# Moving the first layer's expansion matmuls from four-pass float32 to one-pass float32r, with the operand carried through DRAM

## The chip, the core and the metric

The kernel runs on one core of a Trainium2 chip. Its time is the device time of one execution, in microseconds (us). The engines of the core work from separate instruction queues: PE (TensorE, the matmuls), PEld (the loading of a matmul's stationary operand, which can lie beside a matmul), DVE (VectorE), ACT (ScalarE), POOL (GpSimd) and SP (SyncE, which here only issues DMA transfers). SBUF is the on-chip memory of 128 partitions, PSUM the memory that matmuls write to, DRAM the memory outside. The kernel before takes 4007.41 us (median of three runs, 4005.51 to 4009.65).

## The reference

A batch of 8192 samples of 8 x 16 x 16 float32 values goes through four residual layers. Each normalises the samples in groups of two channels, applies a linear map and adds the result to what came in. The change touches layer 0 alone, whose map is a product of three small cores:

```python
def _L0_conv_ref(x, core0, core1, core2, bias):
    ...
    z = x.reshape(b, 1, sin[0], M_rest, 1)
    for k, c in enumerate(cores):
        z = jnp.einsum('bpmqr,rnms->bpnqs', z, c)
        ...
    return z.reshape(batch_shape + tuple(sout)) + bias

def reference(x, ...):
    x = x + _L0_conv_ref(_gn(x), L0_conv_core0, L0_conv_core1, L0_conv_core2, L0_conv_bias)
    x = x + _L1_conv_ref(_gn(x), ...)     # 3x3 convolution, batch norm, relu
    x = x + _L2_conv_ref(_gn(x), ...)     # quantised 3x3 convolution
    x = x + _L3_conv_ref(_gn(x), ...)     # 3x3 convolution with binarised weights
    return x
```

`core2` works on the last axis (16 values in, 16 values and 8 ranks out); `core0` and `core1` together map the other 128 values of a sample and the 8 ranks to 128 values.

## The kernel before

The batch is cut into 64 tiles of 128 samples; a tile is a [128, 2048] float32 array, and is worked on in four quarters of 32 samples. Layers 0 and 1 run together in a first stage of 256 quarters. In it every quarter has three groups of matmuls:

- `expand`, twice: the normalised x (`xn`, 16 rows for the last axis, two samples in 32 partitions) is the stationary operand, and `core2` is streamed past it. Result `pu`, in PSUM, copied by ACT to `u`.
- `main`: eight matmuls of 512 columns over `u`, one for each rank. Result `po`; DVE adds it to x.
- `conv1`: six matmuls of 128 columns, layer 1's convolution for the quarter six earlier. Results `pm` and `pc`.

```python
def expand(t, q, k):                       # before
    if k == 0:
        T[t]["u", q] = us[q % 2].rearrange("p (b n) -> p b n", b=QS)
    pu = ps_u.tile([P, 4, 2, 2 * R * W], F32, ...)          # ps_u holds one such buffer (4 banks)
    xv = T[t]["xn"].rearrange("p (n m) -> p n m", m=CH)
    for j in range(2):
        for i in range(4):
            rows = slice(32 * i, 32 * i + 32)
            pe.matmul(pu[:, i, j], xv[rows, (2 * q + k) * 2 + j],
                      core2[rows].rearrange("p a n -> p (a n)"), start=True, stop=True)
    act.copy(T[t]["u", q][:, 16 * k:16 * k + 16]..., pu...)

def main(t, q, between, n0=None):
    ...
    for r in range(R):                     # R = 8
        for f, args in between.get(r, ()):
            f(*args)                       # other steps, put between the matmuls
        pe.matmul(samples(po)[:, a:b], core01[:, r], u[:, a:b, r, :], start=(r == 0), stop=(r == R - 1))
    dve.tensor_tensor(x[:, cols], po, x[:, cols], ALU.add)

for n in range(NT * NQ):                   # the first stage, a quarter at a time
    ...
    at(0, tn < NT, expand, tn, qn, 0)      # the next quarter's expansion, first half, before matmul r = 0
    at(4, tn < NT, expand, tn, qn, 1)      # and second half, before matmul r = 4
    at1(0, conv1_input, LAG)               # POOL makes conv1's operand
    at1(6, conv1_scaled, LAG - 1)          # ACT's part of it
    if q == 0:
        ... norm_sums, norm_stats of tile t - 1; load_b(t + 3)
    elif q == 1:
        ... norm_b_square of tile t + 2; norm_apply of tile t - 1; load_t(t + 3)
    elif q == 2:
        ... norm_b_sums, norm_b_stats of tile t + 2
    else:
        ... add_bias of tile t + 3; norm_b_spread, norm_b_apply of tile t + 2
    at1(3, conv1_output, LAG + 1)          # DVE puts layer 1's output together
    main(t, q, steps, ...)
    conv1(*quarter_of(n, LAG))
```

Every compute engine keeps the order of the program. `xb` (x in the layout that `expand` needs) is loaded into three buffers `bs`; its normalised form goes to two buffers `xns`. Layer 3, at the end of the kernel, already uses one-pass products: there x is split into `hi` and `lo`, both float32r, and both are multiplied with weights that are exact in that format:

```python
def layer3(i, h):
    for m, t in enumerate(("hi", "lo")):
        for k in range(2):
            ...
            for n in range(3):
                pe.matmul(samples(pc[:, k]), L["sign3"][:, n], tv[:, :, n:n + W], ...)   # 512 columns, rows of 16 out of 18
```

Of the kernel before, what the change touches and what calls it, by code (L numbers as in the profile page):

```python
# [18 lines left out]
P = 128  # L19
C, H, W = 8, 16, 16  # L20
CH = C * H
# [11 lines left out]
class InOrder:  # L33
# [5 lines left out]
    def __getattr__(self, name):  # L39
        op = getattr(self.engine, name)  # L40

        def call(*args, **kwargs):
# [3 lines left out]


PACK0 = [("c0", R * C), ("c1", R * H), ("core2", 2 * R * W), ("bias0", W)]
PACK1 = [("w1", 9 * C), ("linb", C), ("gamma", 1), ("beta", 1), ("w2", 9 * C), ("w2all", C * C * 9), ("bias2", 1),
         ("w3", 9 * C), ("w3all", C * C * 9), ("bias3", 1)]  # L50


@with_exitstack
def tile_net(ctx: ExitStack, tc: tile.TileContext, xb, xt_in, pack0, pack1, out):
    nc = tc.nc
    NT = xt_in.shape[0]

# [3 lines left out]

    x1_d = [dram.tile([P, F], F32, name=f"x1_d{t}", tag=f"x1_d{t}") for t in range(NT)]
    y_d = [dram.tile([P, F], F32, name=f"y_d{t}", tag=f"y_d{t}") for t in range(NT)]
    x2_d = [dram.tile([P, F], F32, name=f"x2_d{t}", tag=f"x2_d{t}") for t in range(NT)]

    def load_pack(src, parts, pool, name):
        t = pool.tile([P, src.shape[1]], F32, name=name)
        nc.scalar.dma_start(t, src)
        views, at = {}, 0
        for key, n in parts:  # L70
            views[key] = t[:, at:at + n]
            at += n
        return views


    hold = ctx.enter_context(tc.tile_pool(name="hold", bufs=1))
    xs, bs, ys, xns, sqs = ([hold.tile([P, F], F32, name=f"{n}{k}") for k in range(m)]
                            for n, m in (("xs", 4), ("bs", 3), ("ys", 2), ("xn", 2), ("sq", 2)))
    us = [hold.tile([P, 2 * F], F32, name=f"u{k}") for k in range(2)]

    STAY = 4
    order2 = list(range(NT - STAY, NT)) + list(range(NT - STAY))
    y_stay = [bs[(NT - 3) % 3], bs[(NT - 2) % 3], bs[(NT - 1) % 3], ys[(NT - 1) % 2]]
    y_of = dict(zip(order2, y_stay))

    x_slots = ([xs[t % 4] for t in order2[:STAY]] + [xns[NT % 2]] + [us[0][:, h * F:(h + 1) * F] for h in range(2)]
               + [xns[(NT - 1) % 2]] + [us[1][:, h * F:(h + 1) * F] for h in range(2)] + y_stay[:3])
    y_slots = [ys[(NT - 1) % 2], ys[NT % 2]] + sqs
    T2 = [dict() for _ in range(NT)]

    def load2(i):
        T2[i]["x"] = x_slots[i % KEEP]
        T2[i]["y"] = y_stay[i] if i < STAY else y_slots[(i - STAY + 1) % len(y_slots)]
        if i >= STAY:
            nc.sync.dma_start(T2[i]["y"], y_d[order2[i]])
            nc.sync.dma_start(T2[i]["x"], x1_d[order2[i]])
# [1 line left out]

    first = ExitStack()
    const1 = first.enter_context(tc.tile_pool(name="const1", bufs=1))  # L100
    w0 = load_pack(pack0, PACK0, const1, "w0")
    ident = const.tile([P, P], F32, name="ident")
    make_identity(nc, ident)
    mhalf = const.tile([P, 64], F32, name="mhalf")
# [22 lines left out]

    core2 = w0["core2"].rearrange("p (a n) -> p a n", a=2)  # L130
    bias0_t = w0["bias0"]
    core01 = const1.tile([P, R, CH], F32, name="core01")
# [1 line left out]

    def late_constants(late):

        w = load_pack(pack1, PACK1, late, "w1")
        yield "load"

        scratch = ys[1]  # L140

        def band(wr, sh, dtype, name):

            acc, tmp = (scratch[:, k * 3 * CH:(k + 1) * 3 * CH].rearrange("p (k h) -> p k h", h=H) for k in range(2))
            b = (const1 if name == "1" else const).tile([P, 3, CH], dtype, name=f"band_{name}", tag=f"band_{name}")
            bv = b.rearrange("p k (c h) -> p (k c) h", c=C)
            wr = wr.rearrange("p (k n) -> p k n", k=3)
            for kh in range(3):
                wv = wr[:, kh, :].unsqueeze(2).to_broadcast([P, 3 * C, H])
                mv = sh[:, kh:kh + H].unsqueeze(1).to_broadcast([P, 3 * C, H])  # L150
                if kh == 0:
                    dve.tensor_tensor(acc, wv, mv, ALU.mult)
                    continue
                dve.tensor_tensor(tmp, wv, mv, ALU.mult)
                dve.tensor_tensor(bv if kh == 2 else acc, acc, tmp, ALU.add)
            L[f"band{name}"] = b

        for k in ("gamma", "beta", "bias2", "bias3"):
            L[k] = const.tile([P, 1], F32, name=k)
# [123 lines left out]
    with first as s:  # L283
# [14 lines left out]
        for t in x1n:  # L298
            pool.memset(t[:, :, 0:W + 2:W + 1], 0.0)

        def load_b(t):
            T[t]["xb"] = bs[t % 3]
            nc.sync.dma_start(T[t]["xb"], xb[t])

        def load_t(t):
# [28 lines left out]
            group_spread(spread0, T[t].pop("mvb"), W)  # L334

        def norm_b_apply(t, q=None):
            src = T[t]["xb"]
            if q in (None, 0):
                T[t]["xn"] = xns[t % 2]
            xn = T[t]["xn"]  # L340
            n = NB // 2 if q is None else NB // NQ
            for k, op, i in ((0, ALU.subtract, src), (1, ALU.mult, xn)):
                for a in range(0, NB, n) if q is None else [q * n]:
                    cols = slice(a, a + n)
                    dve.tensor_tensor(rows_b(xn)[:, cols], rows_b(i)[:, cols],
                                      spread0[:, k, cols].unsqueeze(2).to_broadcast([P, n, 32]), op)

        def expand(t, q, k):

            if k == 0:  # L350
                T[t]["u", q] = us[q % 2].rearrange("p (b n) -> p b n", b=QS)
            pu = ps_u.tile([P, 4, 2, 2 * R * W], F32, name=f"pu_{t}_{q}_{k}", tag="pu")
            xv = T[t]["xn"].rearrange("p (n m) -> p n m", m=CH)
            for j in range(2):
                for i in range(4):
                    rows = slice(32 * i, 32 * i + 32)
                    pe.matmul(pu[:, i, j], xv[rows, (2 * q + k) * 2 + j],
                                     core2[rows].rearrange("p a n -> p (a n)"), start=True, stop=True)
            act.copy(T[t]["u", q][:, 16 * k:16 * k + 16].rearrange("p b n -> p (b n)"),
                           pu.rearrange("p i j n -> p (i j n)"))  # L360

# [128 lines left out]
        def quarter_of(n, lag):  # L490

            t, q = divmod(n - lag, NQ)
            return (t, q) if 0 <= t < NT else None
# [1 line left out]

        load_b(0)
        for t in range(min(3, NT)):
            if t + 1 < min(3, NT):
                load_b(t + 1)
            load_t(t)  # L500
        rest = late_constants(s.enter_context(tc.tile_pool(name="late", bufs=1)))
        next(rest)
        norm_b_square(0)
        norm_b_sums(0)
        c0x = ys[0][:, 0:C * C * H].rearrange("p (n m h) -> p n m h", n=C, m=C)
        pool.tensor_tensor(c0x, w0["c0"].rearrange("p (n m) -> p n m", n=C).unsqueeze(3).to_broadcast([P, C, C, H]),
                           shz[:, 1:H + 1].unsqueeze(1).unsqueeze(1).to_broadcast([P, C, C, H]), ALU.mult)
        norm_b_stats(0)
# [19 lines left out]
        for n in range(NT * NQ):  # L528
# [7 lines left out]
            def at1(r, f, lag):  # L536
                if quarter_of(n, lag):
                    at(r, True, f, *quarter_of(n, lag))
# [15 lines left out]
            if q == 0:  # L554
                if before and t - 1 not in y_of:
                    nc.sync.dma_start(x1_d[t - 1], T[t - 1]["x"])
                at(1, before, norm_sums, t - 1)
                at(4, before, norm_stats, t - 1)
                if t + 3 < NT:
                    load_b(t + 3)  # L560
            elif q == 1:
                at(1, ahead, norm_b_square, t + 2)
                at(1, before, norm_apply, t - 1)
                at(4, t + 3 < NT, load_t, t + 3)
            elif q == 2:
                at(1, ahead, norm_b_sums, t + 2)
                at(1, ahead, norm_b_stats, t + 2)
            else:
                at(1, t + 3 < NT, add_bias, t + 3)
                at(1, ahead, norm_b_spread, t + 2)  # L570
                at(1, ahead, norm_b_apply, t + 2)
            at1(3, conv1_output, LAG + 1)
            if last:
                at(2, q > 1, quarter_apply, t, q - 2)
                at(2, q > 0, quarter_stats, t, q - 1)
            if n >= NT * NQ - 2 and NT > STAY + 2:
                load2(STAY + n - (NT * NQ - 2))
            main(t, q, steps, n0=QS // 2 if n == 0 else None)
            if quarter_of(n, LAG):
                conv1(*quarter_of(n, LAG))  # L580

        t = NT - 1
        conv1_output(t - 1, 1)
# [76 lines left out]

    small = ctx.enter_context(tc.tile_pool(name="small", bufs=4))
    kept = {}
    with tc.tile_pool(name="p2", bufs=2) as p2, tc.tile_pool(name="ps2", bufs=2, space=PSUM) as ps2:
        T = T2
        y_slots += [p2.tile([P, F], F32, name=f"yk{k}", bufs=1) for k in range(4)]
        diag = diagonal("b")
        psc, mask2 = (ps2.tile([P, 96], F32, name=n, tag=n, bufs=1) for n in ("psc2", "mask2"))
# [111 lines left out]
    with ExitStack() as s:  # L781
# [2 lines left out]
        ps_s = s.enter_context(tc.tile_pool(name="ps_s3", bufs=1, space=PSUM))  # L784
        order = sorted(range(NT), key=lambda t: t not in kept)

        sq3, t3, z3 = sqs[0], [sqs[1], ys[0]], [ys[1][:, h * F // 2:(h + 1) * F // 2] for h in range(2)]
        T = [dict() for _ in range(NT)]
        AHEAD = min(NT, KEEP - 6)
        FIRST = 3  # L790
# [218 lines left out]
```

## Time and profile before

| what | value |
|---|---|
| time, median of three | 4007.41 us |
| span of the profiled execution | 4002.5 us |
| PE busy | 3771.8 us (94%) |
| DVE busy | 3386.6 us (85%) |
| POOL busy | 2580.2 us (64%) |
| ACT busy | 2380.6 us (59%) |
| first stage (layers 0 and 1) | from the start to about 2780 us |
| data moved by DMA | 564.48 MB, mean 141 GB/s |

In the profile, lines of the form `out<-in` name the buffers that an instruction writes and reads, with numbers left out. A float32 matmul shows as two records on PE and two on PEld; a float32r matmul, in layer 3, as one. So `pu<-w,xn` with 8192 records is 4096 matmuls. All instructions carry the line of a helper (L43), so they are told apart by the buffers. In the chain of waits a row gives a start, a length, the engine and how many instructions were merged into it.

### The profile page before, as it was taken

To read this page: it belongs to the slowest core of one execution; us is meant where nothing else is said; L and a number is where in the kernel's file an instruction comes from. 1 tells how busy PE (TensorE), PEld (TensorE's weight loads), DVE (VectorE), ACT (ScalarE), POOL (GpSimd) and SP (SyncE) were. 2 spreads that over 40 slices of the span, in tenths; PEclk is the share of its full clock that TensorE was granted. 3 is DMA by queue.
4 is the path that set the end of the run, shared out by engine and by line. 5 is a ranking of instruction groups with operands and counts; after the bars stand their busy time and mean duration, and the time that the engine had idled before them with its cause. 6 is when DMAs were issued, how large, how long until landed. Compare 5 with 4: busy or idle time off the path is not lost.

```text
span 4002.5 us, 55803 instructions
## 1 busy us (share of the span) xinstructions
PE 3771.8 (94%) x20296; PEld 2012.8 (50%) x20358; DVE 3386.6 (85%) x6311; ACT 2380.6 (59%) x2420; POOL 2580.2 (64%) x2597
## 2 busy tenths in 40 slices
PE   8999999999999999999999999998665569999998
PEld 4555555555555555555555555554221135555555
DVE  8888888888888888888888888885999889999997
ACT  4555555555555555555555555554665557777775
POOL 4555555555555555555555555544887759999999
PEclk9999999999999999999999999999777689999999
DMA  3222222222222222222222222213999914444432
GB/s 146 95 95 106 95 95 106 95 95 106 95 95 104 97 95 101 101 95 97 104 95 96 105 95 95 95 54 136 390 424 425 399 42 189 180 179 189 180 148 105
DMA packets 77458, 564.48 MB, mean 141 GB/s; under 512 B 8576, under 2 KB 8704, under 8 KB 8832
## 3 DMA queue, kind: packets, MB, share of 16 engines
q1 hardware_dynamic: 76896, 559.97, 35.8%
q8 instruction: 161, 2.64, 0.3%
q14 instruction: 113, 0.93, 0.1%
q10 hardware_dynamic: 288, 0.94, 0.1%
HBM read 314.47 MB, written 246.42 MB: 140 GB/s over the span
## 4 chain that ended last, share of the span: by engine, by line
PE 86%; DVE 6%; DMA 4%; issue 2%; POOL 1%; ACT 0%; POOLq 0%; DVEq 0%; SPq 0%; ACTq 0%
PE po L43 46%; PE pu L43 14%; PE pf L43 9%; PE pm L43 6%; PE pq L43 4%; PE s L43 3%; PE pc L43 3%; DVE top L43 2%; DMA yk<-y_d 1%; DMA x_d<-u 1%; DMA u<-x_d 1%; DMA x_d<-xs 0%; DMA xs<-x_d 0%; DVE u L43 0%; POOL xs L43 0%
## 5 line engine op out<-in xcount | busy, mean ns | idle before, releaser
L43 PE MATMUL po<-u,core 128*128 128x512 f32 (+1 forms) x4112 | 1895.6, 604 | 1.3 <-DVE xs L43 1.3
L43 ACT COPY u<-pu 128x2048 f32<-128x2048 f32 x512 | 955.6, 1866 | 773.1 <-PE pu L43 773.1
L43 PEld LDWEIGHTS po<-u,core 128*128 128x128 f32 x4112 | 739.8, 190 | 904.5 <-issue 870.4
L43 POOL TENSOR_TENSOR e<-x1n,x 128x512 f32<-128x512 f32 x250 | 302.4, 1209 | 574.7 <-ACT x L43 568.3
L43 PE MATMUL pu<-w,xn 32*128 32x256 f32 x8192 | 587.8, 401 | 4.9 <-DVE xn L43 2.8
L43 DVE TENSOR_TENSOR xs<-po,xs 128x512 f32<-128x512 f32 x256 | 177.1, 692 | 399.4 <-PE po L43 399.4
L43 PEld LDWEIGHTS pu<-w,xn 32*128 32x128 f32 x8192 | 370.4, 184 | 244.6 <-issue 196.0
L43 POOL TENSOR_TENSOR mv<-mv,mhalf 128x4 f32<-128x4 f32 x127 | 129.6, 1020 | 440.7 <-DVE mv L43 440.7
L43 POOL TENSOR_TENSOR v<-e 128x128 f32<-128x128 f32 x750 | 403.1, 552 | 0.0
L43 ACT ACTIVATE m<-pm,b 128x128 f32<-128x128 f32 x250 | 91.9, 368 | 442.6 <-PE pm L43 442.6
L43 PEld LDWEIGHTS pm<-v,fast 128*128 128x128 f32 x2000 | 262.6, 192 | 119.6 <-issue 119.6
L43 POOL TENSOR_TENSOR xs<-xs,w 128x2048 f32<-128x2048 f32 x64 | 291.3, 4553 | 0.0
L43 PE MATMUL pm<-v,fast 128*128 128x128 f32 x2000 | 263.5, 275 | 0.0
L43 ACT ACTIVATE x<-x1n 128x512 f32<-128x512 f32 x500 | 245.3, 542 | 0.0
L43 PE MATMUL pf<-hi,sign 128*128 128x512 f32 x768 | 226.8, 433 | 0.0
L43 PE MATMUL pf<-lo,sign 128*128 128x512 f32 x768 | 219.5, 423 | 3.3 <-ACT lo L43 3.3
L43 POOL TENSOR_TENSOR v<-r 128x128 f32<-128x128 f32 x500 | 219.3, 461 | 0.0
L43 POOL TENSOR_TENSOR mvb<-mvb,mhalf 128x4 f32<-128x4 f32 x64 | 65.2, 1019 | 228.7 <-DVE mvb L43 228.7
L43 ACT ACTIVATE sq<-xs 128x2048 f32<-128x2048 f32 (+1 forms) x107 | 199.1, 1861 | 4.6 <-POOL xs L43 4.6
L43 PE MATMUL gb<-rows_c,sel 128*128 128x128 f32 x128 | 40.4, 409 | 169.8 <-DVE rows_c L43 169.8
L43 PE MATMUL pq<-q,band 128*128 128x480 bf16 (+1 forms) x706 | 188.2, 387 | 10.4 <-ACT q L43 5.2
L43 PEld LDWEIGHTS pf<-hi,sign 128*128 128x128 f32 x768 | 141.4, 191 | 96.6 <-DVE v L43 47.8
(257 smaller groups left out, 6915.3 us busy)
## 6 DMA issues: line engine op xcount, KB each, us to landing
x_d<-xs SPq DMA_DIRECT2D x76, 1024.0 KB, 3.9
bs<-in_xb SPq DMA_DIRECT2D x64, 1024.0 KB, 4.8
xs<-in_xt SPq DMA_DIRECT2D x64, 1024.0 KB, 4.8
y_d<-ys SPq DMA_DIRECT2D x60, 1024.0 KB, 3.9
u<-x_d SPq DMA_DIRECT2D x36, 1024.0 KB, 6.1
xs<-x_d SPq DMA_DIRECT2D x32, 1024.0 KB, 8.9
yk<-y_d SPq DMA_DIRECT2D x29, 1024.0 KB, 19.9
bs<-x_d SPq DMA_DIRECT2D x25, 1024.0 KB, 5.7
```

Source lines behind the costliest of these rows:

```text
L43: return self.tc.keep_in_program_order(op(*args, **kwargs))
```

## The change

Both factors of the expansion, x and `core2`, are each written as the sum of a high half[...] and a low half that holds the rest. The contraction over 32 rows then becomes one over 128 rows: high and low x (each 32 rows) in every second partition and again in the ones between, against high and low `core2`, so that one pass over 128 rows sums all four products of halves. The aim is that PE makes one pass in place of four.

The halves of x start in the 32 partitions in which `xn` lies and have to reach 128 partitions. ACT rounds a quarter to float32r (`xh`), POOL subtracts it from x (the low half, in place), eight transfers of 64 KB from SP write the halves to DRAM, and one transfer of 1 MB from POOL's queue reads them back, each row into two partitions, as float32r (`xl`, two buffers). This is done for tiles 1 to 63; tile 0 keeps the old form.

```diff
+    limb_d = [dram.tile([2, QS, 4 * BANK], F32, ...) for k in range(4)]
+    xls = [const1.tile([P, F], F32R, name=f"xl{k}") for k in range(2)]
...
+        def limbs(t, q):
+            cols = slice(q * BANK, (q + 1) * BANK)
+            x, d = T[t]["xn"][:, cols], limb_d[(t * NQ + q) % len(limb_d)]
+            hi = xh[:, cols].bitcast(F32R)
+            act.copy(hi, x)
+            pool.tensor_tensor(x.bitcast(F32R), x, hi.bitcast(F32), ALU.subtract)
+            for k, half in enumerate((hi.bitcast(F32), x)):
+                for i in range(4):
+                    nc.sync.dma_start(d[k][:, i * BANK:(i + 1) * BANK], half[32 * i:32 * i + 32])
+
+        def fetch(t, q):
+            m = t * NQ + q
+            T[t]["xl", q] = xls[m % 2]
+            d = limb_d[m % len(limb_d)].rearrange("k r n -> (k r) n")
+            pool.dma_start(xls[m % 2], d.unsqueeze(1).to_broadcast([2 * QS, 2, 4 * BANK]))
...
         def expand(t, q, k):
...
+            if t == 0:
+                ...                                   # as before
+            else:
+                xv = T[t]["xl", q].rearrange("p (i n m) -> p i n m", i=4, m=CH)
                 for i in range(4):
-                    rows = slice(32 * i, 32 * i + 32)
-                    pe.matmul(pu[:, i, j], xv[rows, (2 * q + k) * 2 + j], core2[rows]..., ...)
+                    for j in range(2):
+                        pe.matmul(pu[:, i, j], xv[:, i, 2 * k + j], L["core2r"], start=True, stop=True)
...
+            for m, lead in ((4, n == 1), (5, n == 1), (6, n == 2), (n + NQ, n >= 3)):
+                at(2 if n >= 3 else 5, lead and m < NT * NQ, limbs, *divmod(m, NQ))
+            for m in (4, 5) if n == 2 else [n + 3] if n > 2 else []:
+                at(5, m < NT * NQ, fetch, *divmod(m, NQ))
```

In a steady quarter n, then, the halves of quarter n + 4 are made and stored (before matmul r = 2), those of quarter n + 3 are fetched (before r = 5, once both halves of the expansion of quarter n + 1 have read the same buffer), and quarter n + 1 is expanded.

The room for `xh` and `xl` comes from buffers: `bs` has two in place of three and `xns` is gone (x is normalised in place in `bs`), `load_b` loads tile t + 2 in place of t + 3, a part of the later layers' constants (`pack2`) is loaded into `ys`, and the lists of buffers that the second stage reuses are put in another order with the same lengths (13 and 8). Three small DVE operations at the start make `core2r`, the high and low halves of `core2`.

## The prediction

> **What bounds the kernel now.** I read the page's 40 slices first, then the chain of waits, then what the other engines wait for.
>
> ```profile
> PE   8999999999999999999999999998665569999998
> DVE  8888888888888888888888888885999889999997
> PEclk9999999999999999999999999999777689999999
> DMA  3222222222222222222222222213999914444432
> ```
>
> PE is full, at full clock, for the first 28 slices of 100 us: the first stage, which is all that the change touches. DVE is close behind. DMA is mostly idle there, and full in the stage after it, which has its own limit.
>
> The chain of waits in the middle of the first stage (start, length, what):
>
> ```profile
> 1499.36 1.08 PE pu L43 x16
> 1500.43 3.63 PE po L43 x8
> 1504.07 1.08 PE pu L43 x16
> 1505.14 3.63 PE po L43 x8
> 1508.77 0.89 PE pm L43 x8
> 1509.66 0.45 PE pc L43 x4
> ```
>
> This is one quarter, with nothing but PE in it: 2 x 1.08 + 2 x 3.63 + 0.89 + 0.45 = 10.76 us. No wait ends last here, so whatever PE is spared comes off the time until another engine binds. The `pu` rows are not all that an expansion costs. The last quarter of the stage has none, and the chain shows it:
>
> ```profile
> 2757.20 6.87 PE po L43 x16
> 2764.07 0.89 PE pm L43 x8
> 2764.97 0.45 PE pc L43 x4
> ```
>
> Sixteen `po` records take 6.87 us (0.429 each) there, against 7.26 where expansions lie between them. A quarter without expansions is 6.87 + 0.89 + 0.45 = 8.21 us, so the two expansions cost 10.76 - 8.21 = 2.55 us, 1.27 each: 1.08 of their own, and 0.19 that shows up in the first `po` record after them. I take this for the cost of changing between 32-row and 128-row operands, whose loads then don't hide behind the running matmul.
>
> The other engines of this stage, busy us of PE, PEld, DVE, ACT, POOL, then clock, DMA share and GB/s, and DVE's longest wait (total us, times, longest) in 1000 us of the stage:
>
> ```profile
> 100.00:2700.00 2600.00, 2598.69 (x14508) 1405.67 (x14507) 2159.36 (x4183) 1460.10 (x1571) 1432.28 (x2116) 1.00 0.26 97
> ```
>
> ```profile
> DVE xs L43 <- PE po L43: 147.1, 93, 2.4
> ```
>
> Times 10.76/2600, a quarter holds 8.94 us of DVE, 6.04 of ACT and 5.93 of POOL. DVE waits 147.1/93 = 1.6 us per quarter, for PE: it is the next to bind.
>
> What a one-pass product costs is seen in layer 3 (the timeline: start, us, what):
>
> ```profile
> 3561.09 1.71 PE L43 MATMUL pf<-lo,sign 128*128 128x512 f32 x6
> 3562.64 1.72 PE L43 MATMUL pf<-hi,sign 128*128 128x512 f32 x6
> 3564.20 1.20 PE L43 MATMUL pf<-lo,sign 128*128 128x512 f32 x4
> ```
>
> Six of 512 columns take 1.55 to 1.56 us from start to start, 0.259 each.
>
> **What the Trainium skill says.** "FP8 and Floating Point Precision", TensorE Precision Notes: float32 is four passes (the four products of high and low halves), and TensorE natively works at about 22 bits. The trace agrees: a float32 `po` matmul is two records of 0.429 us, 0.858 us for 512 columns, against 0.259 for float32r. But that ratio is 3.3 and not 4. "TensorE: Matmul & The Clock Gate", Part 3: matmuls of 32 rows in different row groups run side by side. The trace agrees: 16 `pu` records of 256 columns, whose two passes would be 0.21 us at the pace of `po` (0.429/2), take 1.08 us and not 3.4. So PE already used all its rows: 8 matmuls x 4 passes / 4 side by side is the same streaming as 8 matmuls x 1 pass. What is to be won is the loss around it. "DMA: Bandwidth & Descriptors", SWDGE vs HWDGE vs iDMA: a transfer into float32r counts as a cast and must be issued from GpSimd, in software. The kernel before has no such transfer; nothing shows its speed. "SBUF — State Buffer", Who interferes with whom: a DVE tensor_tensor with both inputs in SBUF contends with GpSimd's reads. The frequent DVE operations of this stage have one input in PSUM (`po`, `pm`, `pc`, `stat`), so more POOL work should not slow them.
>
> **The change part by part.**
> - Removed: 2 x 1.27 us of PE per quarter, in tiles 1 to 63, 252 quarters.
> - Added on PE: 2 x 8 float32r matmuls of 256 columns per quarter, each with its own load of 128 columns, with no change of row groups before or after. The pace p of one decides all, and nothing in this trace shows it directly. Three readings: (a) p = 0.112, the pace of a `pm` record (0.89/8: also one load of 128 columns and 2 x 128 columns of streaming), if layer 3's 0.259 comes from its rows of 16 out of 18; (b) p = 0.130, if float32r streams four bytes a column at layer 3's rate (0.259 x 256/512); (c) p = 0.152, if layer 3 pays a fixed 0.045 per float32r matmul over half a `po` record (0.259 - 0.429/2), on top of 0.107 for 256 columns (0.429/4). An expansion is then 0.90, 1.04 or 1.22 us in place of 1.27.
> - Per quarter: 0.74, 0.46 or 0.10 us less; over 252 quarters 187, 116 or 25 us. Against (a) speaks that float32 matmuls over the same kind of broken rows show no loss (the `pd` ones, rows of 16 out of 18, start 0.43 apart)[...]. Against (c): the spacings in layer 3 are not constant. I hold (b) for likeliest, then (a), then (c).
> - Added on ACT: a copy of 512 columns to float32r. Layer 3's cast of 2048 takes 1.93 us, one of 256 takes 0.54 us; I put 512 at 0.6. ACT goes from 6.04 to 6.6 us per quarter. It lies between the two copies of `pu` (1.87 us each), at a point where ACT waits up to 2.8 us for PE: hidden.
> - Added on POOL: a subtraction of 512 columns, 1.1 us (layer 3's of 2048 columns takes 4.27), and the issue of one transfer in software, whose cost nothing here shows. POOL goes from 5.93 to 7.0 us plus that issue, which has 3 us before POOL is full. POOL keeps its order, and the fetch waits for PE's second expansion; that comes where POOL waits for ACT's `x4` anyhow (2.1 us in the timeline). Hidden, except perhaps in the quarter with `add_bias` (4.55 us); but `v` is ready some 7 us before `pm` needs it.
> - Added on SP: eight issues of 0.33 us, 2.6 us per quarter; SP has nothing else to do but wait.
> - Added on DMA: 0.5 MB written and 1 MB fetched per quarter, 1.5 MB/10.3 us = 150 GB/s on top of 97. The stage after this reaches 425: there is room. A fetch has the time from matmul r = 5 of quarter n to the start of n + 2, 1.4 quarters or 14 us, less up to 4 where POOL is late; loads of 1 MB land in 4.8 us now.
> - DVE: unchanged, 8.94 us per quarter, against a new quarter of 10.0 to 10.7. It still waits for PE, but by 1.1 us instead of 1.6 or less. PE needs its add of `po` only 1.34 us of `pm` and `pc` and an expansion later, which absorbs uneven quarters.
> - Start and later stages: a few DVE operations more, and the first fetches behind three `add_bias`: 4 us lost. The second and third stages have as many buffers as before: unchanged, about 1220 us.
>
> Sum for (b): 4007 - 116 + 4 = 3895. For (a) 3824, for (c) 3986.
>
> **The rivals.** First, a fixed cost per float32r matmul (c): the layer 3 pace speaks as well for it as for (b); the time would be 3986, no difference worth the name. Second, the fetch becomes the new wait: software-issued, with a cast, to twice the bytes, behind eight small stores that wait for ACT and POOL. For it: nothing shows how fast such a transfer is. Against it: 10 to 14 us of lead. If it took 3 us more than its lead in every quarter, 252 x 3 = 756 us of waits would come on top; in one quarter of four, 189 us, more than the gain. Third, DVE becomes the bound: with (a) the quarter is 10.0 us and DVE 8.94, and where the order of its work pushes the add of `po` late, PE waits. That would leave at most a quarter of 10.2 and 3870. Fourth, `xb` has two buffers: its load starts only when the last halves are stored, and must land in about one quarter; 4.8 us now, perhaps 8 with more traffic: no wait.
>
> **Range and chances.** I weigh (a) 0.25, (b) 0.45, (c) 0.2, and a new wait that eats the gain 0.1. The middle is 3890. Low end: (a) without any loss, 3815. High end: (c) with small stalls, 4000. Faster by over 2% means below 3927: (a), (b) and a little of the rest, 0.62. Slower by over 2% means a fetch that is late in most quarters: 0.11.
>
> **What would show it.** `pu` rows of 8 records in the chain, 0.9, 1.04 or 1.2 us long: the three readings. `po` rows of 3.43 in place of 3.63: no more loss in changing row groups. A quarter of 10.0 to 10.3 us with PE alone in the chain: no new wait. Wrong would be: PE idle before `pu` with a transfer named (the fetch), or before `po` with DVE or ACT; DVE instructions longer than now (POOL in their way); a second stage that starts or runs differently.

## The result, and the profile after

| | us, median | lowest to highest |
|---|---|---|
| before (4 runs) | 4006.46 | 4005.35 to 4009.65 |
| after (4 runs) | 3868.80 | 3868.12 to 3869.61 |

The ratio is 0.9655, with a 95% interval of 0.9639 to 0.9672: 3.4% faster, 138 us. The profiled spans are 4002.5 and 3866.3 us, 136.2 us apart. The 40 slices of the kernel after, of 97 us each:

```profile
PE   7899999999999999999999999996665589999998
DVE  6988888888888888888888888877998889999997
PEclk8999999999999999999999999998776699999999
DMA  5678788787887878878788787757999624444432
```

PE still fills the first stage at full clock. DMA, mostly idle there before, now runs at seven to eight tenths without PE noticing. The first digits of PE and DVE (7 8 and 6 9, where before has 8 9 and 8 8) are the one bad sign: the start has become worse.

The chain of waits in the middle of the stage (start, length, what):

```profile
1504.03 0.94 PE pu L43 x8
1504.97 3.43 PE po L43 x8
1508.40 0.89 PE pm L43 x8
1509.29 0.45 PE pc L43 x4
1509.74 0.94 PE pu L43 x8
1510.67 3.43 PE po L43 x8
```

A quarter is 2 x 0.94 + 2 x 3.43 + 0.89 + 0.45 = 10.08 us, PE alone. The `po` rows have lost their 0.20; a float32r matmul takes 0.94/8 = 0.117 us. From the end of one quarter's DVE add of `po` to the end of the next, averaged over quarters 14 to 250, it is 10.082 us after and 10.751 before: 0.669 us less.

The other engines of the stage (busy us and instructions of PE, PEld, DVE, ACT, POOL, then clock, DMA share, GB/s), DVE's longest wait from 1000 to 2000 us (total us, times, longest), and the fetch among the DMA issues (times, KB each, us from issue to landing):

```profile
100.00:2570.00 2470.00, 2458.50 (x10715) 1526.14 (x10714) 2195.12 (x4218) 1593.47 (x1825) 1897.21 (x2622) 1.00 0.79 258
```

```profile
DVE xs L43 <- PE po L43: 84.1, 99, 1.7
```

```profile
xl<-limb_d POOLq DMA_DIRECT2D x252, 1024.0 KB, 7.4
```

Times 10.08/2470, a quarter holds 8.96 us of DVE, 6.50 of ACT and 7.74 of POOL. DVE waits 84.1/99 = 0.85 us for PE per quarter (1.6 before): it is still not the bound. The fetch lands 7.4 us after its issue, and PE needs it some 14 us after.

Where the 136 us come from, by the ends of DVE's add of `po` and the first `pd` matmul, which opens the second stage:

| part of the span | before, us | after, us | difference |
|---|---|---|---|
| start to the end of quarter 11 | 144.15 | 168.19 | +24.0 |
| quarters 12 to 252 | 2590.95 | 2429.82 | -161.1 |
| quarter 253 to the first `pd` | 30.2 | 29.0 | -1.2 |
| first `pd` to the end | 1237.3 | 1239.4 | +2.1 |

The steady part gains 241 x 0.669 = 161 us. The start gives 24 back, and it should have gained 5 itself (eight quarters, 4 to 11, in the new form at 0.67): 29 us are lost there.

**The start.** The timeline of the kernel after from 33 to 64 us (start, length, engine, what, in brackets the idle time before and what ended it):

```profile
54.24 1.02 POOL L43 TENSOR_TENSOR mvb<-mvb,mhalf 128x4 f32<-128x4 f32 x1 [11.55 <-DVE mvb L43]
...
56.45 1.49 POOL L43 DMA_DIRECT2D xl<-limb_d  x2
...
61.97 2.04 PE L43 MATMUL pu<-core2r,xl 128*128 128x256 f32 x8 [11.30 <-DMA xl<-limb_d]
```

The first fetch is behind tile 2's statistics in POOL's program, and POOL stood 11.55 us waiting for DVE's part of them. The halves lay ready in DRAM; PE then waited 11.30 us for the fetch.

The second loss is in quarters 8 and 9, which take 20.84 and 16.06 us in place of 13.69 and 9.26. DVE is late there. Its timeline after, and the same two operations before:

```profile
110.67 6.50 DVE L43 TENSOR_TENSOR ys<-w,she 128x384 f32<-128x384 f32 x2
...
132.45 5.81 DVE L43 TENSOR_SCALAR quarter<-quarter 128x4 f32<-128x4 f32 x1
```

```profile
79.52 1.49 DVE L43 TENSOR_TENSOR ys<-w,she 128x384 f32<-128x384 f32 x2
...
101.73 0.31 DVE L43 TENSOR_SCALAR quarter<-quarter 128x4 f32<-128x4 f32 x1
```

Two products of 384 columns take 6.50 us in place of 1.49 (5.77 of it the first), and an operation on 4 columns 5.81 in place of 0.31. They make the later layers' constants, and have all their operands in SBUF. In the same time POOL runs one SBUF operation after the other (its timeline after):

```profile
132.72 1.22 POOL L43 TENSOR_TENSOR e<-x1n,x 128x512 f32<-128x512 f32 x1
...
136.28 0.71 POOL L43 TENSOR_TENSOR v<-e 128x256 f32<-128x256 f32 x1
136.96 1.27 POOL L43 TENSOR_TENSOR bs<-bs,xh 128x512 fp32r<-128x512 f32 x1
```

The DVE operation ends at 138.26, and this row of POOL operations at 138.23. The Trainium skill, "SBUF — State Buffer", Who interferes with whom, states that tensor_tensor with both inputs in SBUF contends with GpSimd's reads, and that tensor_scalar can enter a two-port mode, in which whoever issues first has the shared ports for its whole instruction and the other is blocked. The trace agrees as far as it goes (it doesn't show the mode or the ports), and shows more: the small operation lasts over several POOL instructions, not one.

PE's waits are not all that the start loses. After a wait its matmuls run slower for a while: eight `po` records behind a wait of 1.86 us for DVE, at 131.65 us, take 5.40 us, where the rows around it take 3.60. The mean granted clock from 100 to 160 us is 0.89, against 1.00 in the kernel before. How much of the 29 us this makes was not summed.

### The profile page after: what moved, and what is told of

Read it like the earlier page. It is cut to its first block, busy times and chain, and to the rows that moved or that the text cites. A ratio compares the mean times of both kernels' runs of the same rounds, so it can differ in the third digit from the quotient of the medians.

```text
span 3866.3 us, 52820 instructions
## 1 busy us (share of the span) xinstructions
PE 3616.3 (94%) x16326; PEld 2131.0 (55%) x16326; DVE 3408.0 (88%) x6316; ACT 2510.8 (65%) x2672; POOL 3044.2 (79%) x3101
## 4 chain that ended last, share of the span: by engine, by line
PE 84%; DVE 7%; DMA 4%; issue 2%; POOL 1%; ACT 1%; POOLq 0%; DVEq 0%; SPq 0%; ACTq 0%
PE po L43 44%; PE pu L43 12%; PE pf L43 10%; PE pm L43 6%; PE pq L43 4%; PE s L43 3%; PE pc L43 3%; DVE top L43 3%; DMA yk<-y_d 1%; DVE ys L43 1%; DMA x_d<-xs 1%; DMA x_d<-xk 1%; DMA xk<-x_d 1%; DMA xs<-x_d 1%; DMA u<-x_d 1%
## 5 line engine op out<-in xcount | busy, mean ns | idle before, releaser
L43 PE MATMUL po<-u,core 128*128 128x512 f32 (+1 forms) x4112 | 1847.0, 592 | 1.9 <-DVE xs L43 1.9
L43 PE MATMUL pu<-core2r,xl 128*128 128x256 f32 x4032 | 680.1, 311 | 11.3 <-DMA xl<-limb_d 11.3
L43 PEld LDWEIGHTS pu<-core2r,xl 128*128 128x128 f32 x4032 | 529.2, 189 | 134.1 <-issue 133.8
L43 POOL TENSOR_TENSOR bs<-bs,xh 128x512 fp32r<-128x512 f32 (+1 forms) x253 | 324.6, 1283 | 206.0 <-ACT xh L43 206.0
L43 DVE TENSOR_TENSOR bs<-bs,stat 128x1024 f32<-128x1024 f32 x252 | 290.8, 1216 | 2.1
L43 POOL DMA_DIRECT2D xl<-limb_d x252 | 149.7, 594 | 87.5 <-ACT x L43 47.8
```

What stands on the lines that cost most here:

```text
L43: return self.tc.keep_in_program_order(op(*args, **kwargs))
```

## The experiments

Ten kernels ran, each an edit of the kernel after. The first four share a chip and seven runs of the kernel before (4004.89 us, 1.6 under the four above, so differences from after carry some 2 us of doubt). In the tables of quarters, a time is the end of DVE's add of `po`.

**fetch_first.** Only the first two fetches, those in quarter 2, are issued before matmul r = 0, ahead of POOL's wait.

```diff
-                at(5, m < NT * NQ, fetch, *divmod(m, NQ))
+                at(5 if n > 2 else 0, m < NT * NQ, fetch, *divmod(m, NQ))
```

> The first two fetches are issued at the start of quarter 2 (before matmul r = 0) in place of before r = 5. Theory: at the start PE waits 11.3 us for the first fetch only because POOL, which keeps its order, has the fetch behind a statistic of tile 2 that DVE delivers late (POOL waits 11.6 us for it). Then the wait of PE before the first pu of tile 1 falls from 11.3 us to under 2, and the time from 3869 to about 3858. Rival: the halves are stored too late for the fetch to land earlier; then the wait stays over 8 us and the time within 3 us of 3869.

It took 3859.88 us (3857.29 to 3861.98), ratio 0.9637 (0.9623 to 0.9652), 8.9 us less than after. PE's wait before the first new-form matmul is gone:

```profile
51.48 1.18 PE L43 MATMUL pu<-core2r,xl 128*128 128x256 f32 x8 [0.71 <-DMA xl<-limb_d]
```

Quarter 3 ends 13.2 us earlier (61.19 us in place of 74.42), quarter 11 only 7.5: quarter 6 takes 13.45 us in place of 9.72, for DVE. One operation on 8 columns takes 4.78 us there:

```profile
81.01 4.78 DVE L43 TENSOR_SCALAR own<-own 128x8 f32<-128x8 f32 x1
```

It ends 0.03 us after a row of POOL operations that runs from 81.45 to 85.76. So the fetch's place in POOL's order cost 7.5 to 8.9 us of the whole.

**no_extra_step.** The late constants are made in steps, one per quarter (none in a tile's last), and the change puts one more `yield` between them, so that every later step comes a quarter later. This edit removes it; the same operations remain.

```diff
-        yield "limbs"
```

> The step that makes core2r no longer takes a quarter of its own among the late constants, so that the constants after it are made one quarter earlier, as in the kernel before. Theory: quarters 8 and 9 take 20.8 and 16.1 us in place of 10.1 because the last constants fall where POOL already makes conv1's operand, and DVE operations that read SBUF only stand behind POOL's; one quarter earlier they don't meet. Then quarters 8 and 9 together fall from 37 to about 24 us and the time from 3869 to about 3856. Rival: POOL's added work alone keeps DVE, wherever the constants lie; then they stay over 33 us and the time within 4 us of 3869.

3858.76 us (3857.09 to 3863.21), ratio 0.9636 (0.9622 to 0.9651), 10.0 us less. Quarters 8 and 9 take 19.41 and 10.55, together 30.0 where 36.9 were and 24 were hoped for: between the two expectations. Part of the loss was the collision of two steps with one stretch of POOL work: the two operations shown above take 1.41 and 1.86 us here. Quarter 8 stays long because another operation of the late constants now meets such a stretch: a copy of 4 columns takes 5.17 us, where two of them took 1.35 before.

**both.** The two edits together.

> Both edits. If the two losses lie at different places and don't share a cause, their gains add: 3869 - 11 - 13 = 3845. If a quarter that starts earlier only waits longer later (DVE is the bound of the first 12 quarters), it is no better than the better one alone, about 3856.

3850.57 us (3847.86 to 3854.18), ratio 0.9615 (0.9599 to 0.9631): 18.2 less than after, where the two alone sum to 19.0. The losses are separate, and together they are three quarters of the 24 us. (By quarter 11 in the single profiled executions the two alone gain 7.5 and 7.4, and both 18.7: the same within a few us.) What is left in quarter 8 is the same two copies, 5.22 us.

**both_early.** As both, and the halves of the first quarters are made earlier in their quarters.

```diff
-                at(2 if n >= 3 else 5, lead and m < NT * NQ, limbs, *divmod(m, NQ))
+                at(2 if n >= 2 else 1, lead and m < NT * NQ, limbs, *divmod(m, NQ))
```

> Both edits, and the first three sets of halves are made before r = 1 or 2 in place of r = 5. Theory: what is left of PE's wait for the first fetch (a few us) goes as well: 1 to 4 us under the kernel with both edits. Rival: ACT and POOL are late with these at the start, and push DVE's work back: no gain or a loss of a few us.

3850.89 us (3849.13 to 3852.60), ratio 0.9615 (0.9601 to 0.9629): nothing gained, against my theory. Once the fetch is issued in time, it is no longer what the start waits for.

**dense_start.** As both, and the constants advance in every quarter from the first, a tile's last one too.

```diff
-            if n > 0 and q != NQ - 1:
+            if n > 0:
                 next(rest, None)
```

> Both edits at the start, and one step of the late constants in every quarter from the first on (the fourth of a tile too), so that all are made before conv1 begins in quarter 6. Theory: what is left at the start (quarter 8 takes 19.4 us) is DVE making the last constants in operations that read SBUF only, each held up behind POOL's conv1 operand (a copy to 128 x 4 elements takes microseconds there). Made earlier they take tenths; quarter 8 falls to about 11 us and the time from 3851 to about 3843. Rival: DVE is short of time anyway in the first 9 quarters; then the loss only moves to quarters 3 to 6 and the time stays within 3 us of 3851.

3846.00 us (3844.08 to 3849.25; before on that chip 4006.08), ratio 0.9599 (0.9583 to 0.9615). Quarter 8 falls from 19.44 to 10.61 us, but quarter 3 grows from 7.18 to 15.44:

| quarter ends, us | before | after | fetch_first | no_extra_step | both | both_early | dense_start |
|---|---|---|---|---|---|---|---|
| 3 | 60.78 | 74.42 | 61.19 | 73.37 | 60.92 | 61.59 | 69.62 |
| 7 | 99.77 | 110.75 | 102.09 | 110.69 | 99.47 | 103.43 | 106.80 |
| 9 | 122.72 | 147.65 | 139.00 | 140.65 | 129.35 | 131.58 | 127.41 |
| 11 | 144.15 | 168.19 | 160.73 | 160.81 | 149.51 | 151.74 | 148.14 |

The constants of quarter 8 moved, and with them others, which now fall into quarter 3 and meet POOL there:

```profile
55.15 7.80 DVE L43 TENSOR_TENSOR ys<-ys 128x384 f32<-128x384 f32 x1
...
70.90 0.17 DVE L43 TENSOR_SCALAR own<-own 128x8 f32<-128x8 f32 x1
```

The first took 0.56 us before; here POOL has three SBUF operations in a row from 55.53 to 62.53, and these 7.2 us are most of what quarter 3 grew by. The second is the operation that took 4.78 in fetch_first; POOL is idle here from 63.1 to 72.2, and it takes 0.17, with the DMA share at 0.64. So it is not the amount of DVE's work that is too much for the start, as my rival had it, but its meeting with POOL's, and that only moved. At quarter 11 of the profiled execution 1.4 us are left of the gain. By its median this is the fastest of the versions that leave nothing out, and its runs overlap those of both.

**unbroken_rows.** What sets the pace of a float32r matmul: its columns, a fixed cost, or layer 3's rows of 16 out of 18? In layer 3 the moving operand is read as 512 contiguous columns. The convolution multiplies the wrong columns in it.

```diff
-                    tv = T[i][t][:, q * QS:(q + 1) * QS]
+                    tv = T[i][t].rearrange("p b w -> p (b w)")[:, q * QS * (W + 2):(q + 1) * QS * (W + 2)]
...
-                        pe.matmul(samples(pc[:, k]), L["sign3"][:, n], tv[:, :, n:n + W],
+                        pe.matmul(pc[:, k], L["sign3"][:, n], tv[:, 16 * n:16 * n + BANK],
```

> In the changed kernel, layer 3's float32r matmuls read 512 columns in one run in place of 32 rows of 16 out of 18 (the convolution then multiplies the wrong columns). In the first stage a float32r matmul of 256 unbroken columns takes 0.1165 us, 2.2 times less than layer 3's 0.259 for 512. If the broken rows cost (reading a of the prediction), layer 3's six matmuls fall from 1.555 us to 6 x 0.216 = 1.30 or a little more (6 x 0.233 = 1.40 if the small excess of the first stage goes with the columns). If float32r costs by the byte or by the matmul, they stay at 1.55. The time of the whole changes little: layer 3's stage is bound by POOL and DVE.

The timeline of PE in layer 3:

```profile
3500.91 1.56 PE L43 MATMUL pf<-lo,sign 128*128 128x512 f32 x6
3502.31 1.56 PE L43 MATMUL pf<-hi,sign 128*128 128x512 f32 x6
3503.71 1.56 PE L43 MATMUL pf<-lo,sign 128*128 128x512 f32 x6
```

From start to start, six take 1.40 us: 0.233 each, and that is twice the 0.1165 of the expansion's 256 columns. So float32r goes by the column, 0.1165/256 = 0.455 ns, with no fixed part left to see; a float32 `po` record makes 1024 column passes in 0.429 us, 0.419 ns each. Layer 3's 0.259 holds 0.026 for its 32 broken rows. The granted clock is 1.00 in layer 3 in both kernels, so it is not the clock. The kernel took 3858.1 us in its single run, 10.7 less than after, although 1536 matmuls x 0.026 = 40 us of PE were saved: from 3150 to 3840 us POOL is now busy 99% (98% in after) and PE 97% (100%), so the rest is most likely POOL, which now hardly pauses.

**no_traffic.** Halves are made, stored and fetched for the first eight quarters only; later quarters multiply stale halves.

```diff
-                at(2 if n >= 3 else 5, lead and m < NT * NQ, limbs, *divmod(m, NQ))
+                at(2 if n >= 3 else 5, lead and m < 8, limbs, *divmod(m, NQ))
...
-                at(5, m < NT * NQ, fetch, *divmod(m, NQ))
+                at(5, m < 8, fetch, *divmod(m, NQ))
+                if 8 <= m < NT * NQ:
+                    t8, q8 = divmod(m, NQ)
+                    T[t8]["xl", q8] = xls[m % 2]
```

> From quarter 8 on nothing is split, stored or fetched: the expansion reads what the first quarters left in xl. This leaves out all that the change added on ACT, POOL, SP and DMA in the steady state. Theory: all of it is hidden, so the steady quarter stays at 10.08 us and the spacing of pu at 0.117. Rival: the added transfers or the added work slow PE a little (the 0.005 us over a pm record per matmul would be from fetches that write SBUF beside it); then the quarter falls to 10.0.

```profile
1503.30 0.93 PE pu L43 x8
1504.23 3.43 PE po L43 x8
1507.66 0.89 PE pm L43 x8
1508.55 0.45 PE pc L43 x4
1509.00 0.95 PE pu L43 x8
```

The chain in mid stage is the same, and the mean quarter is 10.082 us with and without the ACT copy, the POOL subtraction, the nine transfers and the 1.5 MB per quarter: all of it is hidden there. The whole took 3856.3 us in its single run, 12.5 less than after, and the start has it: quarter 9 ends at 138.31, quarter 11 at 157.38, with the first fetch as late as in after. From quarter 4 on POOL has less to do here, and the two DVE operations are short again:

```profile
112.19 2.40 DVE L43 TENSOR_TENSOR ys<-w,she 128x384 f32<-128x384 f32 x2
...
127.51 0.85 DVE L43 TENSOR_SCALAR quarter<-quarter 128x4 f32<-128x4 f32 x1
```

2.40 and 0.85 us, where after has 6.50 and 5.81. DVE's code is the same. ACT's copy and the DMA transfers went with POOL's work here, so this run alone doesn't single out POOL. The ends do. In the first 200 us of the kernels here, every DVE product of 128x384 that lasts over 1.5 us (eleven of them, up to 7.80) ends 0.41 to 0.43 us after the end of a POOL instruction, every such cast of 128x384 0.22 after one, and every such tensor_scalar of 4 or 8 columns 0.03 to 0.08 after one. They finish as if they began when POOL's instruction ended. Which POOL instruction lets one through is not shown.

**rows32.** Is the gain the changing of row groups? The one-pass matmuls are put on 32 of the 128 rows each, in four row groups in turn, as the old form had them. Three quarters of the contraction are left out.

```diff
-                for i in range(4):
-                    for j in range(2):
-                        pe.matmul(pu[:, i, j], xv[:, i, 2 * k + j], L["core2r"], start=True, stop=True)
+                for j in range(2):
+                    for i in range(4):
+                        rows = slice(32 * i, 32 * i + 32)
+                        pe.matmul(pu[:, i, j], xv[rows, i, 2 * k + j], L["core2r"][rows], start=True, stop=True)
```

> The expansion's one-pass matmuls work on 32 of the 128 rows each, in the four row groups in turn, as before the change; three of the four products of halves are left out. Same count of matmuls, loads and columns. Theory: changing between 32-row and 128-row operands costs about 0.3 us per expansion (a first load that isn't hidden at entry and one at exit, 0.1 each, and one inside), and the streaming is 2 x 0.107: an expansion takes about 0.5 us and the first po record after it is 0.1 longer (po rows of 3.5 or more). Rival: the 0.19 in the po rows of the kernel before came from four-pass float32 and not from the row groups; then po rows stay at 3.43.

```profile
1501.41 3.63 PE po L43 x8
1505.04 0.89 PE pm L43 x8
1505.93 0.45 PE pc L43 x4
1506.38 0.44 PE pu L43 x8
1506.82 3.63 PE po L43 x8
```

`po` is back at 3.63. The quarter is 9.50 us, so an expansion costs (9.50 - 8.21)/2 = 0.65 us. Two rounds of four matmuls, if the four run fully side by side, would stream in 2 x 0.1165 = 0.23; about 0.42 are left for going into row groups and back, more than the 0.3 expected: 0.21 within the `pu` row, 0.20 in the `po` after it. The old form fits the same: four passes of 512 columns at 0.419 ns are 0.86 us, and 0.41 of its 1.27 remain. That the rest is the same where the streaming is 0.23 and where it is 0.86 speaks for a fixed cost of the change, and against four that run only partly side by side. The new form is all streaming: 8 x 0.1165 = 0.93. So the change saves the 0.41 and pays 0.07 for slower columns: 0.34 per expansion, twice that per quarter, where 0.67 was measured.

**seven_ranks.** What binds next? Main makes seven of its eight matmuls; the last rank is left out.

```diff
-                for r in range(R):
+                for r in range(R - 1):
...
-                              start=(r == 0), stop=(r == R - 1))
+                              start=(r == 0), stop=(r == R - 2))
```

> main does seven of its eight matmuls (one rank is left out), which takes 0.858 us of PE from every quarter. If PE still sets the pace alone, the steady quarter falls from 10.08 to 9.22 us. DVE has 8.94 us of work in a quarter and POOL some 7.8; if one of them binds, the quarter stops at a value above 9.3 and waits of PE for DVE or POOL show in the chain. I expect 9.25 to 9.5, with DVE's wait for po nearly gone.

```profile
100.00:2300.00 2200.00, 2168.05 (x9793) 1378.06 (x9794) 2105.50 (x4044) 1522.72 (x1748) 1825.05 (x2513) 1.00 0.84 278
```

```profile
DVE xs L43 <- PE po L43: 4.3, 6, 1.2
...
ACT sq L43 <- DMA bs<-in_xb: 52.8, 27, 4.2
```

The mean quarter is 9.34 us, with stretches at 9.22; 10.08 less one matmul of 0.858 is 9.22. DVE is busy 2105.5/2200 = 96%, and its wait for PE is down from 84.1 to 4.3 us per 1000. So DVE has 0.4 us of room left in a quarter. But it isn't what binds: all that PE waits for from 1000 to 2000 us is ACT, 7.0 us in 6 times. ACT waits for the load of `xb`, 52.8 us in 27 times, once per tile: two buffers begin to show. In the chain of waits over these 1000 us the stores of halves and the loads of `xb` have 7.4%, and no line of DVE more than 0.7%. So the 0.12 us above 9.22 are rather these transfers than DVE, though no run separates them. The whole took 3684.6 us in its single run.

**late_fetch.** How much lead does the fetch need? It is issued a quarter later, for quarter n + 2.

```diff
-            for m in (4, 5) if n == 2 else [n + 3] if n > 2 else []:
+            for m in (4,) if n == 2 else [n + 2] if n > 2 else []:
```

> In quarter n the halves of n + 2 are fetched in place of n + 3: a lead of 0.4 to 0.5 quarters in place of 1.4. A fetch lands 7.4 us after its issue. If the lead is what hides it, PE now waits in every quarter: about 4.4 us from the issue point to the next quarter's expansion, so 3 to 4 us of wait per quarter, more in the quarters where POOL is late with add_bias; a quarter of 13 to 15 us and a time of 4600 to 5100. If a fetch is much faster when PE asks for it alone, the quarter stays near 10.1.

```profile
1514.04 7.18 DMA xl<-limb_d
1521.21 0.14 issue
1521.35 1.17 PE pu L43 x8
```

```profile
PE pu L43 <- DMA xl<-limb_d: 167.2, 62, 5.1
```

4702.1 us in its single run: the transfer's 7.18 us stand in the chain, PE waits for it in 62 of some 74 quarters per 1000 us, and the mean quarter is 13.44. With less lead the change would have cost 17% in place of gaining 3.4%. The waits are 167.2 us per 1000, 2.25 per quarter and less than the 3 to 4 expected. The other 1.1 us above 10.08 are PE's own: it is busy 11.2 us per quarter with the same work, because it is slower after a wait, as in the start of after. The first of these rows of `po` follows a wait of 3.62 us, the second does not:

```profile
1522.36 5.29 PE L43 MATMUL po<-u,core 128*128 128x512 f32 x8
...
1534.14 3.60 PE L43 MATMUL po<-u,core 128*128 128x512 f32 x8
```

The mean granted clock from 1000 to 2000 us is 0.91, where after has 1.00.

## Why the prediction was right, and where it was off

The time predicted was 3890 us, 21 too many, and 3868.8 lies within the range. Two terms of its sum were off, in opposite directions: the gain was 53 us larger than the sum for (b) had, and the loss in the start some 25 larger. That the two cancel in part is luck; the mechanism in the steady part is not.

- **PE alone sets the stage, and what PE is spared comes off.** Right: 161.1 us saved are 241 x 0.669, PE is alone in the chain, and no_traffic gives the same quarter.
- **The expansion costs 1.27, of which 0.19 shows in `po`, for changing row groups.** Right as a cause: 3.43 in place of 3.63, and 3.63 again in rows32. The 0.19 was only half of this cost; it is 0.41 in all, the rest inside `pu`.
- **The pace p of a float32r matmul: (a) 0.112, (b) 0.130, (c) 0.152.** This was the term that decided, and I put most weight on (b). Measured: 0.1165, nearer (a). The argument against (a), that broken rows of 16 out of 18 cost the float32 matmuls nothing, doesn't carry over: they cost float32r 0.026 per 512 columns. The condition of (a), "if layer 3's 0.259 comes from its rows", holds: what goes beyond 0.455 ns a column there is the broken rows. (c), the fixed cost, falls with the same run. The saving per quarter was 0.67 in place of 0.46, over 252 quarters 53 us more than the sum for (b) had.
- **"A few DVE operations more, and the first fetches behind three `add_bias`: 4 us lost."** Wrong in size and in place: 24 us at quarter 11 against before, 29 against what it should have been. I looked for POOL's own work ahead of the fetch, and not for what POOL waits for (11.55 us for DVE). And I took the DVE operations by their durations, not by what a step more does to the order of all later ones. Nor did the sum have the slower matmuls after a wait.
- **ACT 6.6, POOL 7.0 plus the issue, all hidden.** 6.50 and 7.74 us; the issue is 0.594. Hidden in the steady state, as no_traffic shows. The subtraction took 1.28 us, not 1.1.
- **"More POOL work should not slow" DVE, since its frequent operations have an operand in PSUM.** True of these: DVE's 8.96 us per quarter were predicted as 8.94, and the largest operation with one input in PSUM (`bs<-bs,stat`, 1024 columns) stays at 1.22 us. In the start it was wrong, for the rare operations with SBUF operands alone. The page that I cited says so; I applied it to the steady state only.
- **The fetch as the new wait.** It has 14 us and needs 7.4. The rival was a real one: late_fetch, with a quarter less, loses 833 us against after.
- **DVE as the bound.** Not yet: 0.85 us of waits for PE per quarter are its room, and in seven_ranks, at 9.34 us a quarter, 0.4 of it is left.
- **`xb` with two buffers: no wait.** Right at 10.08 us; at 9.3 it starts to appear.
- **Later stages unchanged.** 2.1 us more after the first `pd`.
- **The range and the chances.** Two figures don't follow from their terms: (a) without any loss is 4007 - 187 = 3820, not 3815, and (a) and (b) together have 0.70, more than the 0.62 given for a time under 3927.

Sum by the terms as measured: -161.1 in the steady part, +24.0 in the start, +0.9 in the rest, -136.2 of span.

## What to carry to other kernels

Where a small-row matmul uses all rows through row groups, packing its passes into the contraction saves no streaming; it saves the changes between row groups, some 0.4 us per block, and where PE alone sets the stage, as here, that was worth 6% of it. Data that must cross partitions can go through DRAM at no cost in time if its lead exceeds the transfer by a margin, so settle the lead before the arithmetic; and a transfer issued from a compute engine's queue inherits every wait ahead of it in that queue. A change of the steady state is paid in the start: read the first ten iterations apart from the mean.

## What the runs showed of the hardware

- float32r costs 0.455 ns per column (0.1165 us for 256, 0.233 for 512), against 0.419 per column and pass of float32: a ratio of 3.7 for the whole product, not 4.
- Reading 512 columns as 32 rows of 16 out of 18 costs a float32r matmul 0.026 us more (0.259 against 0.233); float32 matmuls over such rows start 0.43 apart per record, as over whole ones.
- A block of eight matmuls in 32-row groups between matmuls of 128 rows costs about 0.42 us besides its streaming, half of it in the matmuls after it.
- A DVE operation on 128x4 elements took 5.81 us in place of 0.31 while POOL worked without a pause in SBUF, and 0.85 with less POOL work. One on 128x8 took 4.78 us beside a row of POOL operations, and 0.17 with POOL idle. The long ones end at a fixed time after a POOL instruction (0.03 to 0.08 us for these, 0.41 to 0.43 for products of 128x384).
- After a wait of 3.62 us for a transfer, a row of eight `po` records took 5.29 us in place of 3.60.
- A transfer of 1 MB that POOL issues, cast to float32r with each row to two partitions, takes 0.594 us of POOL and lands in 7.4 us; the 64 KB stores that SP issues land in 4.3 (`xh`) and 5.1 (`bs`) us.
